# One block for a batch's graph products, and sums of exponentials by accumulating DMAs, in a two-layer graph network on one core

## The chip, the core and the metric

The kernel runs on one core of a Trainium2 chip. A core has TensorE (PE in the profile; its weight loads are PEld), VectorE (DVE), ScalarE (ACT), GpSimd (POOL), SyncE (SP), which here only issues DMAs, and 16 DMA engines that serve the queues of SP, POOL and ACT. The metric is the device time of one launch in microseconds (us), the median of several runs.

## The reference

Inputs are x (16 batches of 1024 nodes with 256 features), an adjacency of 1024 x 1024, and weights, all float32. Layer 0, for each batch, with 4 heads of 64:

```
c_adj = mean over features of x                       # one number per node
A     = | |sigmoid(c_j - c_i) - 0.5| - 0.5 | * 2      # symmetrised
g     = relu(x^T @ (adj * A) * para)                  # 256 x 1024: the queries
k, v  = x @ kv_w
out   = softmax(q k^T * scale) v                      # per head, 1024 x 1024 scores
x     = layernorm(x + out)
```

Layer 1 multiplies by a normalised adjacency, then two linear layers with batch norms and a ReLU, adds x and normalises. Nothing of layer 1 is touched by the change.

## The kernel before, in words

Layer 0 runs over 16 batches. For each batch PE does four kinds of work.

Keys and values. Four steps of values and four of keys, from x transposed.

Graph products. The product of x^T and the weights wg (1024 x 1024, held as eight tiles of 128 rows) is made as a 2 x 2 block product with seven half-size products instead of eight (a Strassen form); batch 0 alone does it plainly. Each of p1 to p7 (line 883) is four matmuls of 128 x 128 by 512, which the profile shows as eight, since each float32 matmul is two instructions. The left factors are sums of quarters of x, kept in two slots of the tile S (`left_first`, `left_third`, `left_last`, lines 849 to 859). The right factors are differences of quarters of wg, made in place by `right(1)` to `right(4)` (line 869), four DVE instructions each, so that a difference must wait until the products that want the old values have read them. Products 1 and 2 accumulate in the PSUM tile pga, 6, 7 and 4 in pgb, 3 in pgd, 5 in pgc; DVE and ACT combine them in qT, weigh them by para and rectify them.

Attention. A batch has 32 units: two pairs of heads, two halves of the queries, eight blocks m of keys. One unit is `scores` (line 1051: matmuls of 64 x 64 into a PSUM tile ps), an exponential on ACT into an SBUF tile p (line 1056, four buffers), and `outputs` (line 1072: matmuls of 64 x 64 that accumulate over the eight m in two PSUM tiles po). `outputs` also adds p to the running sum acc on DVE: line 1080 for the first two, line 1082 for the other six, so seven additions for the eight blocks. After m = 7, ACT copies the first po to oT (line 1089), DVE adds the second (line 1090), DVE transposes oT in blocks of 32 (line 1101), and SP stores it and loads it back in rows (`squares`, `squares_to_rows`).

The end of a batch. For each pair of heads `normalise` sums acc over partitions by matmuls with ones (den, line 1120; shape 128 x 32), ACT copies den (line 1126), and SP stores and reloads it as columns. `residual` takes the reciprocal on DVE (line 1141), multiplies o by it and adds it to x on POOL (lines 1147 and 1148). Then come the statistics of the layernorm on DVE (`statistics_x1`), its application on ACT (`finish_x1`), and a store of x by POOL.

The order is written by hand for PE, ACT, DVE and SP: every instruction of these engines stands in the queue as the program emits it. POOL is ordered by the scheduler. Units go in bursts of two, 16 bursts (u = 0 to 15) to a batch. In each, PE does the scores of this burst, then `back`, the outputs of the burst before; after that comes what is put at that u: at u = 0 seven of the eight key and value steps of the next batch, with the side work for its weights (`weights_abs`, `weights_tanh` on ACT, `weights_adj` on DVE) in between, and den of the batch before's second pair; at u = 4 products 1, 3 and 2 of the next batch, with the last step of its keys; at u = 5 to 7 the differences of the weights (`between`); at u = 8 products 6, 7, 5, 4 with den of the first pair; from u = 9 on, loads and side work for the batch after. `full` holds residuals, `late` the layernorm, `rows_of` the loads of o, `sums` the calls of `normalise`, and `run` emits the next few of a list.

PSUM has three tags with two buffers each: s (ps, two banks a buffer), t (one bank; pga to pgd, keys, values, den) and o (one bank; po). SBUF tiles are in pools; xS is a pool of one buffer for x in squares and, before, for S as well.

Of the kernel before, what the change touches and what calls it, by code (L numbers as in the profile page):

```python
# [515 lines left out]
def fast_path(  # L516
# [216 lines left out]
    with (  # L733
        tc.tile_pool(name="l0c", bufs=1) as l0c,
        tc.tile_pool(name="qkv", bufs=2) as qkv,
        tc.tile_pool(name="pp", bufs=4) as pp,
        tc.tile_pool(name="accp", bufs=2) as accp,
        tc.tile_pool(name="rdp", bufs=1) as rdp,
        tc.tile_pool(name="op", bufs=2) as op,
        tc.tile_pool(name="osp", bufs=1) as osp,  # L740
# [42 lines left out]
        def prologue(b):  # L783
# [65 lines left out]
            def left_first():  # L849
                s2, s4 = s["S"][:, 0], s["S"][:, 1]  # L850
                nc.vector.tensor_tensor(s2, A21, A22, ALU.add)
                nc.vector.tensor_tensor(s2, s2, A11, ALU.subtract)
                nc.vector.tensor_tensor(s4, A12, s2, ALU.subtract)
# [7 lines left out]
            def right(k):  # L861
                for i in KC:
# [38 lines left out]
            def p1():  # L901
                s["qT"] = qkv.tile([P, CC, N], F32, tag="qT", name=f"qT_{b}")
                s["S"] = xsp.tile([P, 2, NCH // 2, P], F32, tag="xS", name=f"S_{b}")
                pg["a"] = tile_t(f"pga_{b}")
                product(1, pg["a"], True)
                nc.scalar.copy(q_at(1, H0), pg["a"])  # L906
                left_first()
                right(1)

            def p3():  # L910
# [3 lines left out]

            def p2():
# [4 lines left out]
            def between(u):  # L920
                right(u - 3)
                if u == 6:
                    nc.vector.tensor_add(q_at(0, H1), q_at(0, H1), q_at(1, H0))
                if u == 7:
                    left_third()

            def p6():
                pg["b"] = tile_t(f"pgb_{b}")
                product(6, pg["b"], True)
                nc.vector.tensor_add(q_at(0, H1), pg["b"], q_at(0, H1))  # L930
                left_last()

            def p7():
                product(7, pg["b"], False)
                nc.vector.tensor_add(q_at(1, H1), pg["b"], q_at(1, H0))

            def p5():
# [6 lines left out]

            def p4():
# [73 lines left out]
            else:  # L1019
                a, t, j = weights_abs, weights_tanh, weights_adj  # L1020
                side += [(f, (n,)) for f, n in (
                    (a, 0), (t, 0), (a, 1), (t, 1), (a, 2), (t, 2), (a, 3),
                    (t, 3), (a, 4), (t, 4), (j, 0), (a, 5), (t, 5), (j, 1),
                    (a, 6), (j, 2), (j, 3), (t, 6), (j, 4), (a, 7), (j, 5),
                    (t, 7), (j, 6), (j, 7),
                )]
            if b:
                s["graph"] = dict(
                    between=between, p=(None, p1, p2, p3, p4, p5, p6, p7),
# [13 lines left out]
        def scores(i):  # L1043
# [11 lines left out]
            p = pp.tile([P, N], F32, tag="p", name=f"p_{i}")  # L1055
# [3 lines left out]
        def outputs(i):  # L1059
# [16 lines left out]
            def sums():  # L1076
                if m == 0:
                    g["p0"] = p
                elif m == 1:
                    nc.vector.tensor_add(g["acc"], g.pop("p0"), p)  # L1080
                else:
                    nc.vector.tensor_add(g["acc"], g["acc"], p)  # L1082

            if i < len(units) - 1:
                sums()
            if m == NCH - 1:
                k = (b * PAIRS + pr) * 2 + qh
                g["oT"] = op.tile([P, HALF], F32, tag="oT", name=f"oT_{k}")
# [49 lines left out]
        def residual(b, pr, qh):  # L1138
# [5 lines left out]
            if (b, pr) != (B - 1, PAIRS - 1):  # L1144
                o = g["o"].rearrange("p n q d -> p n (q d)")
                oh = o.rearrange("p n (h d) -> p n h d", d=D)
                nc.gpsimd.tensor_tensor(oh, oh, r, ALU.mult)  # L1147
                nc.gpsimd.tensor_tensor(xs, xs, o, ALU.add)  # L1148
# [34 lines left out]
        scr = const.tile([P, P], F32, name="scr")  # L1183
# [34 lines left out]
        def adjacency_diagonal():  # L1218
            for n in range(NCH):
# [90 lines left out]
        with tc.manual_schedule(  # L1310
# [70 lines left out]
            for j in range(len(bursts)):  # L1381
# [3 lines left out]
                if u == 0:  # L1385
                    steps, side = next_steps, next_side
                    next_first, next_steps, next_side = [], [], []
                if j:
                    back(j - 1)
                if u in (5, 9, 13):  # L1390
                    run(rows_of, 1)
                if u == 5 and b + 2 < B:
                    load_x(b + 2)
                    next_first, next_steps, next_side = prologue(b + 2)
# [10 lines left out]
                elif u == 0:  # L1405
                    for i in range(7):
                        if b:
                            run(steps, 1)
                            run(side, (2, 3, 2, 3, 2, 2, 99)[i])
# [3 lines left out]
                elif u < 4:  # L1413
                    if u == 1:
                        run(full, 2)
                    else:
                        run(late, 1)
                    run(side, 99)
                elif u == 4:
                    p = st[b + 1]["graph"]["p"]  # L1420
                    keys_last = steps[:1] if b else []
                    del steps[: len(keys_last)]
                    p[1]()
# [625 lines left out]
```

## Time and profile before

| | |
|---|---|
| time, median of 3 runs | 2445.71 us (2445.69 to 2445.86) |
| the profiled execution | 2446.41 us, its span 2444.6 us |
| granted TensorE clock | 0.997 |
| PE busy | 2411.5 us, 99% of the span |
| DVE busy | 1862.8 us, 76% |
| ACT busy | 1238.3 us, 51% |
| POOL busy | 475.7 us, 19% |
| POOL's DMA queue | 50.34 MB, 4.9% of 16 engines |

A line of a group names the line of code, the engine, the operation, what it writes and reads, the shapes and the count; then the busy time and the mean of one in ns; then the idle time of the engine just before, and what ended most of it. A line of the timeline gives the start in us from the span's start, the duration, the engine, line, operation and tiles, how many equal instructions are merged, and in brackets the idle time before with its releaser. The end of a matmul is modelled, so PE's pace is read from one start to the next. Idle time of an engine that is not the bottleneck costs nothing.

### The profile page before, as it was taken

What the parts mean: (1) busy time and instruction counts of PE and PEld (TensorE: products, weight loads), DVE (VectorE), ACT (ScalarE), POOL (GpSimd) and SP (SyncE); (2) the same over time, 40 slices, a digit from 0 to 9 for tenths busy, and PEclk for the clock granted to TensorE, in tenths of its full rate; (3) what the DMA queues carried; (4) which work ended last, traced back from release to release, by engine and by line L of the source; (5) the groups of instructions that cost most, each with busy time, mean ns of one, the idle gap of its engine ahead of it and who ended that gap; (6) DMA issues with size and microseconds to landing.
All of it is one profiled execution on the core that took longest, in us unless ns stands there. A gap on an engine that the chain in (4) does not pass through costs nothing.

```text
span 2444.6 us, 32834 instructions
## 1 busy us (share of the span) xinstructions
PE 2411.5 (99%) x12422; PEld 1029.6 (42%) x12422; DVE 1862.8 (76%) x2570; ACT 1238.3 (51%) x1545; POOL 475.7 (19%) x486
## 2 busy tenths in 40 slices
PE   9999999999999999999999999999999999999997
PEld 5343443443434434434334343344444444444455
DVE  5688878878888888788788888956566566478978
ACT  7376675765765756657647667421110111045568
POOL 0021122111311211122112112422122122010026
PEclk9999999999999999999999999999999999999999
DMA  5124232332232332322322327221222222165559
GB/s 164 40 42 85 57 49 70 70 53 68 38 83 54 48 84 56 53 70 56 63 62 44 83 49 97 82 103 70 96 92 78 94 86 86 69 241 172 172 210 343
DMA packets 423175, 221.99 MB, mean 91 GB/s; under 512 B 361568, under 2 KB 394848, under 8 KB 414560
## 3 DMA queue, kind: packets, MB, share of 16 engines
q1 hardware_dynamic: 417648, 168.94, 28.4%
q0 software_dynamic: 4832, 50.34, 4.9%
q8 instruction: 99, 1.62, 0.3%
q14 instruction: 68, 0.56, 0.1%
q10 hardware_dynamic: 528, 0.52, 0.1%
HBM read 136.06 MB, written 83.69 MB: 90 GB/s over the span
## 4 chain that ended last, share of the span: by engine, by line
PE 86%; DVE 9%; ACT 3%; DMA 1%; issue 1%; POOL 0%; POOLq 0%; DVEq 0%
PE ps L1051 18%; PE po L1072 18%; PE pgb L883 7%; PE b_agg L1556 4%; PE pga L883 4%; PE c_agg L1556 4%; PE pk L980 4%; PE b_o L1763 3%; PE pv L993 3%; PE a_agg L1556 2%; PE b_h L1588 2%; PE pgd L883 2%; PE pgc L883 2%; PE a_o L1763 2%; PE c_o L1763 2%; PE c_h L1588 2%
## 5 line engine op out<-in xcount | busy, mean ns | idle before, releaser
L1056 ACT ACTIVATE p<-ps 128x1024 f32<-128x1024 f32 x512 | 497.6, 1021 | 183.7 <-PE ps L1051 130.1
L1082 DVE TENSOR_TENSOR acc<-acc,p 128x1024 f32<-128x1024 f32 x384 | 500.1, 1302 | 54.2 <-ACT p L1056 29.3
L1051 PE MATMUL ps<-qT,kT 64*64 64x512 f32 x4096 | 488.1, 592 | 0.3 <-ACT p L1056 0.3
L1072 PE MATMUL po<-p,v 64*64 64x512 f32 x4096 | 485.3, 589 | 0.0
L1147 POOL TENSOR_TENSOR o<-o,r_all 128x512 f32<-128x512 f32 x62 | 94.8, 1538 | 1090.8 <-DVE r_all L1141 1052.5
L1072 PEld LDWEIGHTS po<-p,v 64*64 64x64 f32 x4096 | 158.2, 133 | 281.3 <-issue 274.3
L1051 PEld LDWEIGHTS ps<-qT,kT 64*64 64x64 f32 x4096 | 151.4, 133 | 286.8 <-issue 249.2
L834 DVE SCALAR_TENSOR_TENSOR wg<-wg,adj_s 128x1024 f32<-128x1024 f32 x128 | 149.4, 1217 | 16.5 <-ACT wg L830 16.5
L825 ACT ACTIVATE wg<-crow,ccol 128x1024 f32<-128x1024 f32 x128 | 146.8, 1147 | 0.5 <-DMA crow<-c 0.5
L830 ACT ACTIVATE wg<-wg 128x1024 f32<-128x1024 f32 x128 | 136.0, 1062 | 0.9
L980 PE MATMUL pk<-xT,kvw_s 128*128 128x512 f32 x256 | 121.8, 598 | 3.1 <-ACT drow L1126 3.1
L993 PE MATMUL pv<-kvw_s,xT 128*128 128x256 f32 x512 | 124.0, 385 | 0.0
L993 PEld LDWEIGHTS pv<-kvw_s,xT 128*128 128x128 f32 x512 | 94.9, 190 | 50.0 <-issue 13.4
L893 ACT ACTIVATE qT<-qT 128x512 f32<-128x512 f32 x60 | 37.3, 629 | 149.8 <-DVE qT L896 145.2
L883 PE MATMUL pgb<-wg,S 128*128 128x512 f32 x240 | 111.0, 605 | 0.0
L883 PE MATMUL pga<-wg,x 128*128 128x512 f32 x240 | 109.6, 599 | 0.7 <-ACT qT L906 0.7
L1556 PE MATMUL a_agg<-ahT,x1l 128*128 128x512 f32 x240 | 108.1, 593 | 0.7 <-ACT agg L1298 0.7
L1148 POOL TENSOR_TENSOR x<-x,o 128x512 f32<-128x512 f32 x62 | 107.8, 1748 | 2.3
L1556 PE MATMUL b_agg<-aT,x1S 128*128 128x512 f32 x240 | 107.9, 592 | 0.0
L654 ACT COPY p_agg<-a_agg 128x512 f32<-128x512 f32 x15 | 8.8, 586 | 183.3 <-PE a_agg L1556 183.3
L690 POOL TENSOR_TENSOR x1S<-x1l 128x512 f32<-128x512 f32 x15 | 19.0, 1264 | 352.3 <-PE c_agg L1556 349.0
L1080 DVE TENSOR_TENSOR acc<-p,p 128x1024 f32<-128x1024 f32 x64 | 77.4, 1209 | 7.5 <-ACT p L1056 7.5
(230 smaller groups left out, 3511.8 us busy)
## 6 DMA issues: line engine op xcount, KB each, us to landing
h<-hw POOLq DMA_DIRECT2D x16, 2048.0 KB, 6.7
hl<-h SPq DMA_DIRECT2D x32, 1024.0 KB
x<-x POOLq DMA_DIRECT2D x16, 1024.0 KB, 4.2
x1l<-x SPq DMA_DIRECT2D x16, 1024.0 KB
xf<-x SPq DMA_DIRECT2D x16, 1024.0 KB
o<-oS SPq DMA_DIRECT2D x62, 256.0 KB
o<-o SPq DMA_DIRECT2D x248, 64.0 KB
x<-in_x_dram SPq DMA_DIRECT2D x15, 1024.0 KB
```

The source lines that it names most:

```text
L825: nc.scalar.activation(w, s["crow"], AF.Abs, bias=s["ccol"][:, n : n + 1])
L830: nc.scalar.activation(w, w, AF.Tanh, scale=0.5)
L834: nc.vector.scalar_tensor_tensor(w, w, 1.0, adj_s[:, n, :], op0=ALU.subtract, op1=ALU.mult)
L883: nc.tensor.matmul(ps, left, right, start=(start and i == 0), stop=(i == NCH // 2 - 1), skip_group_check=True,)
L980: nc.tensor.matmul(ps, kvw_s[:, c, kc * P : (kc + 1) * P], s["xT"][:, c, hs], start=(c == 0), stop=(c == CC - 1),)
L993: nc.tensor.matmul(pt[:, j * C : (j + 1) * C], s["xT"][:, c, n * P : (n + 1) * P], kvw_s[:, c, C : 2 * C], start=(c == 0), stop=(c == CC - 1),
L1051: nc.tensor.matmul(ps[kh * D : (kh + 1) * D, hd * HALF : (hd + 1) * HALF], kT[r, pr, ks], qT[r, pr, qh * HALF : (qh + 1) * HALF], start=Tr ...
L1056: nc.scalar.activation(p, ps, AF.Exp)
L1072: nc.tensor.matmul(g["po"][kh][hd * D : (hd + 1) * D, :], s["v"][r, m, h * D : (h + 1) * D], p[r, hd * HALF : (hd + 1) * HALF], start=(m = ...
L1082: nc.vector.tensor_add(g["acc"], g["acc"], p)
L1556: nc.tensor.matmul(ps, left, right, start=(start and i == 0), stop=(i == NCH // 2 - 1), skip_group_check=True,)
L1763: nc.tensor.matmul(ps, left, right, start=(start and i == 0), stop=(i == 1), skip_group_check=True,)
```

## The change

It does four things.

- The seven graph products stand in one block at u = 4, in the order 1, 3, 2, 6, 7, 5, 4. The differences that stood at u = 5 to 7 are made in the block, the first sums of x at the end of u = 0, and two of the four differences of `right(1)` at u = 1. pga and pgb take PSUM buffers of the tag o instead of t.
- Of each group's eight tiles p, that of m = 2 lies in a pool of its own (ppb, one buffer) and takes the sums: the tiles of m = 4 and 5 are added to it by DMAs that POOL issues (`accum_op`), and it is added to acc after m = 7. So DVE does five additions in a group instead of seven.
- The residual's multiplication goes from POOL to DVE, and its addition to x is made by an accumulating DMA on POOL's queue.
- Work around these is moved: den of the first pair from u = 8 to u = 9, ahead of that burst's outputs; the load of x for the batch after next and its first step (`begin`, the column sums) from u = 5 and u = 8 to the end of u = 4 and to u = 5; the first pair's residuals from u = 11 to u = 13; the rows of o from u = 13 to u = 15; and the side work for weights is ordered anew. oT gets a pool of one buffer, and a scratch tile shares one with den's row.

```diff
@@ left_first
+                s["S"] = xsp.tile([P, 2, NCH // 2, P], F32, tag="xS", name=f"S_{b}")
                 s2, s4 = s["S"][:, 0], s["S"][:, 1]
@@ right
-            def right(k):
-                for i in KC:
+            def right(k, rows=KC):
+                for i in rows:
@@ the products
-            def p1():
+            def first_three():
                 s["qT"] = qkv.tile([P, CC, N], F32, tag="qT", name=f"qT_{b}")
-                s["S"] = xsp.tile([P, 2, NCH // 2, P], F32, tag="xS", name=f"S_{b}")
-                pg["a"] = tile_t(f"pga_{b}")
+                pg["a"] = tile_o(f"pga_{b}")
                 product(1, pg["a"], True)
                 nc.scalar.copy(q_at(1, H0), pg["a"])
-                left_first()
-                right(1)
-
-            def p3():
+                right(1, KC[2:])
                 pg["d"] = tile_t(f"pgd_{b}")
                 product(3, pg["d"], True)
                 nc.scalar.copy(q_at(0, H1), pg["d"])
-
-            def p2():
+                right(2)
                 product(2, pg["a"], False)
                 nc.vector.tensor_mul(q_at(0, H0), pg["a"], para_s[:, 0, H0])
                 rectify(0, H0)
-            def between(u):
-                right(u - 3)
-                if u == 6:
-                    nc.vector.tensor_add(q_at(0, H1), q_at(0, H1), q_at(1, H0))
-                if u == 7:
-                    left_third()
             def p6():
-                pg["b"] = tile_t(f"pgb_{b}")
+                left_third()
+                right(3)
+                nc.vector.tensor_add(q_at(0, H1), q_at(0, H1), q_at(1, H0))
+                pg["b"] = tile_o(f"pgb_{b}")
                 product(6, pg["b"], True)
                 nc.vector.tensor_add(q_at(0, H1), pg["b"], q_at(0, H1))
                 left_last()
-            def p7():
+                right(4)
+            def last_three():
                 product(7, pg["b"], False)
...
@@ side work of batches from 2 on
-                    (a, 0), (t, 0), (a, 1), (t, 1), (a, 2), (t, 2), (a, 3),
-                    (t, 3), (a, 4), (t, 4), (j, 0), (a, 5), (t, 5), (j, 1),
-                    (a, 6), (j, 2), (j, 3), (t, 6), (j, 4), (a, 7), (j, 5),
-                    (t, 7), (j, 6), (j, 7),
+                    (a, 0), (t, 0), (j, 0), (a, 1), (t, 1), (j, 1), (a, 2), (t, 2),
+                    (a, 3), (t, 3), (j, 2), (a, 4), (t, 4), (a, 5), (j, 3), (t, 5),
+                    (j, 4), (a, 6), (t, 6), (j, 5), (a, 7), (t, 7), (j, 6), (j, 7),
@@ scores
-            p = pp.tile([P, N], F32, tag="p", name=f"p_{i}")
+            pool, tag = (ppb, "pb") if m == 2 else (pp, "p")
+            p = pool.tile([P, N], F32, tag=tag, name=f"p_{i}")
@@ sums, in outputs
+                elif m == 2:
+                    g["pb"] = p
+                elif m in (4, 5):
+                    nc.gpsimd.dma_start(g["pb"], p, accum_op=ALU.add)
                 else:
                     nc.vector.tensor_add(g["acc"], g["acc"], p)
+                if m == NCH - 1:
+                    nc.vector.tensor_add(g["acc"], g["acc"], g.pop("pb"))
@@ residual
-                nc.gpsimd.tensor_tensor(oh, oh, r, ALU.mult)
-                nc.gpsimd.tensor_tensor(xs, xs, o, ALU.add)
+                nc.vector.tensor_tensor(oh, oh, r, ALU.mult)
+                nc.gpsimd.dma_start(xs, o, accum_op=ALU.add)
@@ the bursts
+                if u == 9 and b < B - 1:
+                    run(sums, 1)
                 if j:
                     back(j - 1)
-                if u in (5, 9, 13):
+                if u in ((5, 9, 13) if b == B - 1 else (5, 9, 15)):
                     run(rows_of, 1)
-                if u == 5 and b + 2 < B:
-                    load_x(b + 2)
-                    next_first, next_steps, next_side = prologue(b + 2)
...
-                            run(side, (2, 3, 2, 3, 2, 2, 99)[i])
+                            run(side, (2, 2, 2, 2, 2, 2, 99)[i])
...
+                    st[b + 1]["graph"]["left"]()
                 elif u == 4:
                     p = st[b + 1]["graph"]["p"]
...
+                    p[0]()
                     run(late, 2)
...
+                    p[1]()
+                    if b:
+                        run(steps, 1)
+                    p[2]()
+                    if b + 2 < B:
+                        load_x(b + 2)
+                        next_first, next_steps, next_side = prologue(b + 2)
+                elif u < 4:
+                    if u == 1:
+                        run(full, 2)
+                        st[b + 1]["graph"]["right"](1, range(2))
+                    else:
+                        run(late, 1)
+                elif u == 5:
+                    run(next_first, 1)
+                elif u > 8:
...
-                    if u == 11:
-                        run(full, 2)
...
+                    if u == 13:
+                        run(full, 2)
...
-                    run(next_side, 1)
+                    run(next_side, 2 if u in (11, 13) else 1)
```

More of the change, by code (lines that the diff above doesn't have):

```diff
@@ L736, in fast_path @@
         tc.tile_pool(name="pp", bufs=4) as pp,
+        tc.tile_pool(name="ppb", bufs=1) as ppb,
         tc.tile_pool(name="accp", bufs=2) as accp,
@@ L739, in fast_path @@
         tc.tile_pool(name="op", bufs=2) as op,
+        tc.tile_pool(name="otp", bufs=1) as otp,
         tc.tile_pool(name="osp", bufs=1) as osp,
@@ L931, in p6 @@
                 left_last()
-            def p7():
+                right(4)
+            def last_three():
                 product(7, pg["b"], False)
                 nc.vector.tensor_add(q_at(1, H1), pg["b"], q_at(1, H0))
-            def p5():
                 pg["c"] = tile_t(f"pgc_{b}")
@@ L943, in p5 @@
                     weigh(c, H1)
-            def p4():
                 product(4, pg["b"], False)
@@ L1028, in prologue @@
                 s["graph"] = dict(
-                    between=between, p=(None, p1, p2, p3, p4, p5, p6, p7),
+                    left=left_first, right=right, p=(first_three, p6, last_three),
                 )
@@ L1087, in outputs @@
                 k = (b * PAIRS + pr) * 2 + qh
-                g["oT"] = op.tile([P, HALF], F32, tag="oT", name=f"oT_{k}")
+                very_last = k == 4 * B - 1
+                pool, tag = (op, "o") if very_last else (otp, "oT")
+                g["oT"] = pool.tile([P, HALF], F32, tag=tag, name=f"oT_{k}")
                 nc.scalar.copy(g["oT"], g["po"][0])
@@ L1182, in fast_path @@
         rows, diag, colsum, deg, dinv = dg[:, 0], dg[:, 1], dg[:, 2], dg[:, 4], ncol[:, 0, :NCH]
-        scr = const.tile([P, P], F32, name="scr")
         def load_weights():
@@ L1218, in adjacency_diagonal @@
         def adjacency_diagonal():
+            scr = rdp.tile([P, P], F32, tag="drow", name="scr")
             for n in range(NCH):
@@ L1412, in fast_path @@
                             run(rows_of, 1)
-                elif u < 4:
-                    if u == 1:
-                        run(full, 2)
-                    else:
-                        run(late, 1)
-                    run(side, 99)
+                    st[b + 1]["graph"]["left"]()
                 elif u == 4:
                     p = st[b + 1]["graph"]["p"]
-                    keys_last = steps[:1] if b else []
-                    del steps[: len(keys_last)]
-                    p[1]()
-                    run(keys_last, 1)
+                    p[0]()
                     run(late, 2)
-                    p[2]()
-                    p[3]()
-                elif u == 8:
-                    p = st[b + 1]["graph"]["p"]
-                    p[6]()
-                    run(next_first, 1)
-                    run(sums, 1)
                     if b == B - 2:
@@ L1436, in fast_path @@
                             adjacency_rows(n)
-                    p[7]()
-                    p[5]()
-                    p[4]()
-                elif u < 8:
-                    st[b + 1]["graph"]["between"](u)
-                else:
+                    p[1]()
[14 more added lines that the diff above has]
+                elif u > 8:
                     if u == 9 and b + 2 < B:
                         load_squares(b + 2, 0)
-                    if u == 11:
-                        run(full, 2)
                     if u == 12:
```

## The prediction

> **What bounds the kernel now.** I read the page first, then the timelines of PE and ACT around one graph block, then the releases behind PE's few gaps. The page: busy time by engine, and two groups.
>
> ```profile
> PE 2411.5 (99%) x12422; PEld 1029.6 (42%) x12422; DVE 1862.8 (76%) x2570; ACT 1238.3 (51%) x1545; POOL 475.7 (19%) x486
> ...
> L1082 DVE TENSOR_TENSOR acc<-acc,p 128x1024 f32<-128x1024 f32 x384 | 500.1, 1302 | 54.2 <-ACT p L1056 29.3
> L1147 POOL TENSOR_TENSOR o<-o,r_all 128x512 f32<-128x512 f32 x62 | 94.8, 1538 | 1090.8 <-DVE r_all L1141 1052.5
> L1148 POOL TENSOR_TENSOR x<-x,o 128x512 f32<-128x512 f32 x62 | 107.8, 1748 | 2.3
> ```
>
> PE is busy for 2411.5 of 2444.6 us. DVE has 582 us spare, so work taken off it pays only where PE now waits for it. Next, PE's timeline in the seventh batch, then ACT's over the same microseconds.
>
> ```profile
> 656.75 1.90 PE L1051 MATMUL ps<-qT,kT 64*64 64x512 f32 x16
> 658.47 1.90 PE L1072 MATMUL po<-p,v 64*64 64x512 f32 x16
> 660.30 3.70 PE L883 MATMUL pga<-wg,x 128*128 128x512 f32 x8
> 663.83 1.88 PE L980 MATMUL pk<-xT,kvw_s 128*128 128x512 f32 x4
> ...
> 684.58 1.90 PE L1072 MATMUL po<-p,v 64*64 64x512 f32 x16
> 686.40 3.70 PE L883 MATMUL pgb<-wg,S 128*128 128x512 f32 x8
> 690.04 1.06 PE L1120 MATMUL den<-acc,ones 128*32 128x512 f32 x8
> 691.03 3.70 PE L883 MATMUL pgb<-wg,S 128*128 128x512 f32 x8
> ```
>
> ```profile
> 658.41 1.03 ACT L1056 ACTIVATE p<-ps 128x1024 f32<-128x1024 f32 x1 [2.05 <-DVE acc L1082]
> 659.74 1.02 ACT L1056 ACTIVATE p<-ps 128x1024 f32<-128x1024 f32 x1 [0.30 <-DVE acc L1082]
> 660.66 0.58 ACT L1089 COPY oT<-po 128x512 f32<-128x512 f32 x1
> ...
> 686.53 0.59 ACT L1089 COPY oT<-po 128x512 f32<-128x512 f32 x1 [0.62 <-PE po L1072]
> ```
>
> A product of the graph (8 matmuls) lasts 3.43 us, a start each 0.429; a unit's scores or outputs 0.86. PE runs through without a gap; it loses time only where the tile shape changes. By the starts, the step from po (64x64) to pga (128x128) is 0.519 where 0.429 is usual, and the second matmul after it comes 0.533 after the first: 0.194 for entering. Leaving (pgd to ps) shows 0.522 and a second start 0.03 late: 0.124. A batch takes 96.69 us, and about 1.5 of it is of this kind. The other fact is in ACT's lines: the copy that empties the first po bank ends at 661.24, when pga has been running for 0.94 us. Today nobody waits for it, because pga lies in a bank of its own. One more gap recurs in 14 batches: PE at pk, for the copy of den.
>
> ```profile
> 637.65 1.14 ACT L825 ACTIVATE wg<-crow,ccol 128x1024 f32<-128x1024 f32 x1
> 638.69 0.57 ACT L1126 COPY drow<-den 128x512 f32<-128x512 f32 x1
> ```
> ```profile
> 639.32 1.12 PE L980 MATMUL pk<-xT,kvw_s 128*128 128x512 f32 x2 [0.23 <-ACT drow L1126]
> ```
>
> **What the Trainium skill says.** TensorEngine Tiling (Array Packing), Key Properties: changing the tiling mode drains TensorE. The trace agrees: 0.09 at the step, 0.03 to 0.10 at the next. DMA: Bandwidth & Descriptors, Anatomy of one DMA: a transfer issued from GpSimd costs about 2.0 us plus bytes over 436 GB/s. The trace's 1 MB store of x (POOL) lands after 4.24 us (formula 4.4), the 2 MB store of h after 6.6. The same page, Two DMAs through the same engine are not ordered: a second DMA on the same bytes must wait for the first one's semaphore. So the two accumulations into pb run one after the other. Collectives: The Full Stack, The bandwidth ceiling: a reducing transfer reads two sources and got half the rate of a copy (32 against 62 GB/s). No run here shows an accumulating DMA.
>
> **The change, part by part** (batches 0 to 14 have a graph block).
>
> 1. One block instead of two. One entry and one exit go: 0.194 + 0.124 = 0.318, times 15: **-4.8**.
>
> 2. den of the first pair leaves the block (0.093 in, 0.093 + 0.104 out = 0.29) and goes between scores and outputs of the tenth burst. The last batch has it there already: 0.09 in, 0.093 + 0.03 out = 0.21. Times 15: **-1.2**.
>
> 3. pga and pgb go to the tag of po, whose two banks hold the group just finished. The first product cannot start before ACT has copied po's first bank. In the seventh batch that copy ends 0.94 us after pga starts now, 0.71 where ACT is not behind (686.53 + 0.59 against 686.40), and PE starts 0.05 after a release (drow 639.26, pk 639.32). So PE stands 0.76 to 1.0 us at each block. What would hide it, the next burst's scores, comes after the block. pgb needs the second bank, freed by DVE (L1090) some 4 us later, but is first written three products in, at 10.3: hidden. I take 0.85, since DVE has two sums fewer to be behind with: 15 x 0.85 = **+12.8**.
>
> 4. The differences of weights and rows (L869, 0.61 us each when chained) move from bursts 6 to 8 into the block. DVE enters at most 5.2 us after its start (oS ends at 665.57); right(1)'s rest and right(2), 6 x 0.61, end near 9.5, and the fourth product wants them at 10.3. Then DVE waits for the third product's end (10.4), multiplies, and runs left_third, right(3), two additions: 8 operations, 5.0 us, to 15.5. The fifth product (P7) overwrites pgb and may start then; PE gets there after P6 and the keys at 13.7 + 1.7 = 15.4. So 0.1 x 14, and 1.8 in batch 0, which has no keys left: **+3.3**. left_last and right(4) end by 19, ahead of 18.9 + 0.43 and 22.3: hidden. left_first, now ahead of the second burst, lies beside the key and value products.
>
> 5. The weights' order at the batch's start: ahead of drow's copy ACT has three activations (t3, a4, t4) where it had four (t3, a4, t4, a5), one of 1.14 us less. The 0.23 gap (0.174 of pitch and a 0.104 hitch) goes: 14 x 0.28 = **-3.9**.
>
> 6. Sums: DVE loses m = 2, 4, 5 and gains one addition of pb, so 2 x 1.30 x 64 = 167 us less, off the path. POOL gets two DMAs of 512 KB per group. Take t = 0 at the scores of m = 4. Its exponential ends at 2.17; the first DMA lands at 2.2 + L, the second at 2.3 + 2L. Wanted: p's buffer for the next group's second exponential (four in rotation; natural start 8.9), and pb added before L1090, so that the next group's outputs find both banks at 12.0: 2.3 + 2L + 1.25 + 0.65 + 0.05 under 12.0, L under 3.8. A plain copy by the trace's line through 1 and 2 MB is 1.9 + 1.17 = 3.1: no wait. At half the rate 1.9 + 2.34 = 4.2 (estimate from that line and the skill's half): 12.65 against 12.0 at the bank, 0.65 at two groups of a batch (the other two have a block behind them), and up to 1.1 with the buffer. Below nothing it cannot be: PE gains nothing from DVE's slack here. I take **0** in the forecast, and up to +50 for the range.
>
> 7. Residual: POOL's 1.54 and 1.75 us go, DVE gets 0.69 (x62, as L1090) ahead of which it waits for o and the reciprocals; xs grows by a DMA in 512-byte runs. The statistics a burst (3.43 us) later wait for it; DVE already waits 1.16 us there for POOL. If it lands after 5 us, DVE is 1.5 us later, and the buffers of p catch that while it has two sums less: **0**.
>
> 8. SP: the load of x moves behind the block's last product in program order. The x it overwrites is stored after eight activations (4.7 us), which now follow the third product: 12 + 4.7 + 4.3, then 5.6 for the load (675.75 to 681.3 now) ends 27 us into the block; csum (2.28, DVE) asks at about 28.7. Hidden with under 2 us to spare; late, it holds all sums queued on DVE. At the tenth burst SP has den and dcol (about 5 us), then o, then the squares, which so come one to two bursts later; their 128-byte packets run beside the third group's accumulations: a risk for item 6.
>
> Sum: -4.8 - 1.2 + 12.8 + 3.3 - 3.9 = **+6.2** on a span of 2444.6 (the profiled run took 2446.41, 0.7 above the median shown). On the median 2445.71: **2452**, 0.25% slower; own range 2449 to 2458.
>
> **The rivals.** Accumulations land late (0.32): L near 4.2. For it, the two source reads; against it, that SBUF is both source and target. 31 groups at 0.65 give +20; with the buffer's wait, which also delays the copy of item 3 by 1.2, about +50: 2464 to 2505, 2478 in the middle. Late and crowded (0.08): the third and fourth groups share the engines with the squares and o, L over 5: 2520.
>
> Not slower (0.13): the wait of item 3 is at its floor. Place: the copy at the block's head. If the exponentials ahead of it no longer wait for DVE (2.05 and 0.30 above) it costs 0.76, 11.4 in all, and if DVE also reaches P7 in time, 1.4 more goes: +3.4, 2449. It decides at 0.77 us per block, where the sum crosses 4.9 us. Faster (0.05): the same, with entries that lose their 0.104 hitch, (1.6) comes to +1.8; it takes something that I do not see.
>
> **How the numbers follow.** 0.2% is 4.9 us, about what a measurement of this kernel can tell from no change. Forecast 0.42, of which 0.12 lies under 2450.6. Same: 0.13 + 0.12 = 0.25. Slower: 0.30 + 0.32 + 0.08 = 0.70. Faster 0.05. The range 2444 to 2500 leaves out the 0.05 below and the crowded case with the end of the late one, about 0.15.
>
> **What the profile after would show.** One graph block of 28 products' matmul pairs per batch, its first matmul released by ACT's copy of po after 0.8 to 1.0 us (item 3); PE at pk without drow (5); P7 released by DVE within 0.2 (4); p's DMAs landing in 3.1 us and no PE wait behind L1090 or an exponential (6). I am wrong if these land near or over 4 us, if DVE waits for x at csum, or if the copy is no wait at all.

## The result, and the profile after

The changed kernel takes 3022.94 us (median of 4 runs, 3020.63 to 3023.78) against 2445.72 for the kernel before: 1.2358 times as long, with a 95% interval of 1.2337 to 1.2380. Slower was right. The size, 577 us where 6 were forecast and 54 was the end of the range, was not.

The page of the kernel after: busy time by engine, three of the groups, and the two accumulating DMAs (KB of one, then the median us from issue to landing).

```profile
PE 2557.5 (85%) x12422; PEld 1062.3 (35%) x12422; DVE 1735.8 (57%) x2504; ACT 1241.7 (41%) x1545; POOL 453.5 (15%) x552
...
L1047 ACT ACTIVATE p<-ps 128x1024 f32<-128x1024 f32 x512 | 507.8, 1023 | 710.2 <-DMA p<-p 528.0
L1079 DVE TENSOR_TENSOR acc<-acc,p 128x1024 f32<-128x1024 f32 x64 | 78.4, 1225 | 432.1 <-DMA p<-p 432.0
...
L886 PE MATMUL pga<-wg,x 128*128 128x512 f32 x240 | 144.2, 756 | 187.3 <-ACT oT L1088 187.3
...
p<-p POOLq DMA_DIRECT2D x128, 512.0 KB, 5.4
...
x<-o POOLq DMA_DIRECT2D x62, 256.0 KB, 5.5
```

DVE is less busy, as the change wants (1735.8 us, 1862.8 before). But PE has fallen from 99% of the span to 85%, and the two engines behind it wait for the new DMAs: ACT 528.0 us ahead of its exponentials, DVE 432.0 us ahead of the addition of pb. The same DMAs take 5.4 us from issue to landing, where the forecast had 3.1.

How a wait of ACT comes to PE is seen at the block of the seventh batch. PE's timeline, with its idle time in brackets, then ACT's.

```profile
873.29 1.90 PE L1063 MATMUL po<-p,v 64*64 64x512 f32 x16
888.17 5.31 PE L886 MATMUL pga<-wg,x 128*128 128x512 f32 x8 [12.98 <-ACT oT L1088]
```
```profile
877.37 1.02 ACT L1047 ACTIVATE p<-ps 128x1024 f32<-128x1024 f32 x1 [5.03 <-DMA p<-p]
886.62 1.02 ACT L1047 ACTIVATE p<-ps 128x1024 f32<-128x1024 f32 x1 [8.23 <-DMA p<-p]
887.54 0.58 ACT L1088 COPY oT<-po 128x512 f32<-128x512 f32 x1
```

ACT's queue is in order. The second exponential of the next group wants the buffer of p that the second DMA is still reading, so it stands for 8.23 us; the copy that empties po is queued behind it, and the block is queued on PE behind that copy. PE stands 12.98 us. The row of pga above shows the sum of this over 15 blocks, 187.3 us. Two more of PE's waits (total, times, longest) make up nearly all the rest of its idle time:

```profile
PE ps L1041 <- ACT p L1047: 149.7, 36, 5.9
PE den L1119 <- DVE v L989: 72.6, 14, 7.2
```

The first are scores behind exponentials that wait for a DMA. The second come from the wait of DVE: the addition of pb stands in its queue, ahead of the copy of v that den's place in PSUM waits for (at the start of the seventh batch DVE waits 7.01 us for the DMA, and PE then 4.67 at den). Two more waits at den, for pb's addition itself, add 14.3 us.

POOL's timeline over the same microseconds, and at the next group of that batch, shows why the second DMA is so late.

```profile
868.33 2.60 POOL L1147 DMA_DIRECT2D x<-o  x2 [26.81 <-DVE r_all L1140]
869.93 1.92 POOL L1075 DMA_DIRECT2D p<-p  x1
877.21 1.11 POOL L591 TENSOR_SCALAR rs_l<-mv_l 128x8 f32<-128x8 f32 x1 [5.37 <-DVE mv_l L619]
878.41 2.69 POOL L593 TENSOR_TENSOR rs_l<-rs_l,mhalf 128x8 f32<-128x8 f32 x1
...
881.94 0.92 POOL L1075 DMA_DIRECT2D p<-p  x1 [0.22 <-issue]
```
```profile
922.84 0.87 POOL L1075 DMA_DIRECT2D p<-p  x1 [16.28 <-ACT p L1047]
929.71 0.87 POOL L1075 DMA_DIRECT2D p<-p  x1 [6.00 <-DMA p<-p]
```

In the first group the first DMA is issued right behind two residual DMAs and lands at 877.26, after 7.33 us. The second is then held by four small operations of the layernorm on POOL, which wait for DVE's statistics: issued at 881.94, landed at 886.51, after 4.57. In the second group nothing stands in POOL's queue, and it is late all the same: the scores of m = 4 start at 919.52, the first DMA goes out 3.3 us later and lands at 928.82, the second goes out 0.9 after that and lands at 935.73, 16.2 us after the scores.

Last, the same block in stretches: us, busy time by engine (with counts), granted TensorE clock, DMA share, GB/s.

```profile
862.80:875.50 12.70, 12.39 (x116) 4.03 (x108) 10.82 (x23) 5.87 (x6) 3.51 (x3) 1.00 0.50 66
875.50:888.30 12.80, 0.13 (x1) 0.13 (x1) 5.23 (x11) 2.52 (x3) 5.17 (x5) 0.59 0.31 58
888.30:900.00 11.70, 11.70 (x24) 5.19 (x25) 5.19 (x8) 1.17 (x2) 0.00 (x0) 0.87 0.06 22
```

The clock falls to 0.59 while PE stands and is still below 1 after it (0.87 on average in the third stretch): the first four steps between matmuls are 1.015, 0.854, 0.853 and 0.710 us where 0.429 is usual. The Trainium skill describes this (TensorE: Matmul & The Clock Gate, What's actually happening): after an idle window of about 3.4 us the array gets half its clock pulses, until it has been busy for as long again. The trace agrees, with half pace for about 3 us after this long stand. Outside such stretches the DMAs do not slow the matmuls: 710 of the steps within graph products in this kernel are 0.42 to 0.44 us as before, and 56 about 0.85.

Over layer 0's attention as a whole (first scores to the first product of layer 1), PE's idle time ahead of matmuls, in gaps over 0.05 us, is added up from the trace; the rest is work, at the clock granted. Each kernel's span is within 10 us of what these differences say, so they are where the time is.

| | stage, us | idle, us | gaps over 2 us | rest, us | clock |
|---|---|---|---|---|---|
| before | 1496.8 | 4.1 | 0 | 1492.7 | 1.00 |
| after | 2066.9 | 429.4 | 64 | 1637.5 | 0.887 |
| after without the DMAs of p (next section) | 1523.8 | 25.9 | 2 | 1497.9 | 0.998 |

### The profile page after: what moved, and what is told of

It is laid out like the page before. It is cut to its first block, busy times and chain, and to the rows that moved or that the text cites. A ratio compares the mean times of both kernels' runs of the same rounds, so it can differ in the third digit from the quotient of the medians.

```text
span 3021.4 us, 32826 instructions
## 1 busy us (share of the span) xinstructions
PE 2557.5 (85%) x12422; PEld 1062.3 (35%) x12422; DVE 1735.8 (57%) x2504; ACT 1241.7 (41%) x1545; POOL 453.5 (15%) x552
## 4 chain that ended last, share of the span: by engine, by line
PE 42%; DMA 19%; issue 16%; DVE 10%; ACT 4%; POOL 2%; SPq 2%; POOLq 0%; ACTq 0%; DVEq 0%
DMA p<-p 13%; PE pgb L886 5%; PE pga L886 4%; PE b_agg L1549 4%; PE c_agg L1549 3%; PE ps L1041 3%; ACT p L1047 3%; DMA x<-o 3%; PE po L1063 3%; PE b_o L1756 2%; PE a_agg L1549 2%; PE b_h L1581 2%; DMA o<-o 2%; PE pgc L886 2%; PE c_o L1756 2%
## 5 line engine op out<-in xcount | busy, mean ns | idle before, releaser
L1047 ACT ACTIVATE p<-ps 128x1024 f32<-128x1024 f32 x512 | 507.8, 1023 | 710.2 <-DMA p<-p 528.0
L1041 PE MATMUL ps<-qT,kT 64*64 64x512 f32 x4096 | 528.3, 623 | 149.8 <-ACT p L1047 149.7
L1063 PE MATMUL po<-p,v 64*64 64x512 f32 x4096 | 518.5, 620 | 1.1 <-DVE oT L1089 1.1
L1079 DVE TENSOR_TENSOR acc<-acc,p 128x1024 f32<-128x1024 f32 x64 | 78.4, 1225 | 432.1 <-DMA p<-p 432.0
L886 PE MATMUL pga<-wg,x 128*128 128x512 f32 x240 | 144.2, 756 | 187.3 <-ACT oT L1088 187.3
L1077 DVE TENSOR_TENSOR acc<-acc,p 128x1024 f32<-128x1024 f32 x192 | 233.4, 1216 | 80.6 <-ACT p L1047 72.6
L1075 POOL DMA_DIRECT2D p<-p x128 | 131.0, 1023 | 862.5 <-ACT p L1047 575.2
L1147 POOL DMA_DIRECT2D x<-o x62 | 81.4, 1552 | 542.6 <-DVE r_all L1140 470.1
L886 PEld LDWEIGHTS pga<-wg,x 128*128 128x128 f32 x240 | 57.5, 247 | 271.3 <-ACT oT L1088 200.6
L984 PE MATMUL pv<-kvw_s,xT 128*128 128x256 f32 x512 | 142.0, 426 | 0.0
L1119 PE MATMUL den<-acc,ones 128*32 128x512 f32 x248 | 61.0, 1030 | 86.8 <-DVE v L989 72.6
L872 DVE TENSOR_TENSOR wg<-wg,wg 128x512 f32<-128x512 f32 x120 | 78.9, 688 | 72.3 <-PE pgd L886 72.3
```

The lines of the kernel that those rows point to most:

```text
L886: nc.tensor.matmul(ps, left, right, start=(start and i == 0), stop=(i == NCH // 2 - 1), skip_group_check=True,)
L984: nc.tensor.matmul(pt[:, j * C : (j + 1) * C], s["xT"][:, c, n * P : (n + 1) * P], kvw_s[:, c, C : 2 * C], start=(c == 0), stop=(c == CC - 1),
L1041: nc.tensor.matmul(ps[kh * D : (kh + 1) * D, hd * HALF : (hd + 1) * HALF], kT[r, pr, ks], qT[r, pr, qh * HALF : (qh + 1) * HALF], start=Tr ...
L1047: nc.scalar.activation(p, ps, AF.Exp)
L1063: nc.tensor.matmul(g["po"][kh][hd * D : (hd + 1) * D, :], s["v"][r, m, h * D : (h + 1) * D], p[r, hd * HALF : (hd + 1) * HALF], start=(m = ...
L1075: nc.gpsimd.dma_start(g["pb"], p, accum_op=ALU.add)
```

## The experiments

My theory after the result: nearly all of it is the accumulations of p, through landings that come later than wanted, and half-pace matmuls after each stand. The rivals: the block itself costs far more than was summed (items 3 and 4); the residual's DMA does it (item 7), by crowding POOL's queue; or each DMA costs PE time whatever its deadline.

| kernel | median, us | ratio to before, 95% interval |
|---|---|---|
| block alone | 2559.58 | 1.0463 (1.0449 to 1.0478) |
| block, DMA of the residual | 2547.26 | 1.0414 (1.0398 to 1.0430) |
| block, DMAs of p | 3050.15 | 1.2467 (1.2448 to 1.2486) |
| before, DMAs of p | 2881.11 | 1.1778 (1.1760 to 1.1796) |
| before, DMA of the residual | 2455.32 | 1.0033 (1.0021 to 1.0046) |
| after, no sums of m = 4 and 5 | 2476.26 | 1.0122 (1.0106 to 1.0137) |
| the same, pga in the tag t | 2466.49 | 1.0079 (1.0063 to 1.0094) |
| after, plain copies for accumulations | 2616.30 | 1.0693 (1.0673 to 1.0712) |
| after, one DMA a group | 2653.19 | 1.0841 (1.0825 to 1.0858) |
| after, POOL in program order | 2967.09 | 1.2126 (1.2107 to 1.2145) |
| after, DMAs of m = 1 and 3 | 2943.71 | 1.2007 (1.1971 to 1.2043) |
| before, one early DMA a group | 2563.69 | 1.0468 (1.0450 to 1.0486) |
| after, one early DMA a group | 2718.30 | 1.1095 (1.1076 to 1.1115) |
| before, new order of the weights' work | 2441.90 | 0.9981 (0.9973 to 0.9988) |
| the same, den at the tenth burst | 2463.08 | 1.0067 (1.0054 to 1.0081) |

### The DMAs apart from the block

The block alone puts seven additions back on DVE and the residual's addition on POOL:

```diff
-                elif m == 2:
-                    g["pb"] = p
-                elif m in (4, 5):
-                    nc.gpsimd.dma_start(g["pb"], p, accum_op=ALU.add)
                 else:
                     nc.vector.tensor_add(g["acc"], g["acc"], p)
-                if m == NCH - 1:
-                    nc.vector.tensor_add(g["acc"], g["acc"], g.pop("pb"))
...
-                nc.vector.tensor_tensor(oh, oh, r, ALU.mult)
-                nc.gpsimd.dma_start(xs, o, accum_op=ALU.add)
+                nc.gpsimd.tensor_tensor(oh, oh, r, ALU.mult)
+                nc.gpsimd.tensor_tensor(xs, xs, o, ALU.add)
```

> The changed kernel with both kinds of accumulating DMA undone (all seven sums on DVE, the residual on POOL): the one block and the moved work alone. Theory DMA (the loss comes from the accumulations of p, each over 4.5 us, two in series, which hold p's buffers and the sum pb): 2440 to 2458, my steps 1 to 5 give 2452. Theory block (PE's wait for po's bank at the block's head, and DVE's work crowded into the block, is the loss by itself): over 2600, with the 12 us wait before pga still there.

It takes 114 us more than before, a miss. The block is not nearly free when DVE keeps its sums. The seventh batch's first group, DVE, then ACT, then POOL:

```profile
692.50 2.09 DVE L871 TENSOR_TENSOR wg<-wg 128x512 f32<-128x512 f32 x2
694.51 4.27 DVE L1071 TENSOR_TENSOR acc<-acc,p 128x1024 f32<-128x1024 f32 x2
```
```profile
692.49 1.94 ACT L1045 ACTIVATE p<-ps 128x1024 f32<-128x1024 f32 x2 [2.71 <-DVE acc L1069]
696.66 1.02 ACT L1045 ACTIVATE p<-ps 128x1024 f32<-128x1024 f32 x1 [2.23 <-DVE acc L1071]
```
```profile
692.64 2.84 POOL L1138 TENSOR_TENSOR o<-o,r_all 128x512 f32<-128x512 f32 x2 [22.80 <-DVE r_all L1132]
695.45 4.45 POOL L1139 TENSOR_TENSOR x<-x,o 128x512 f32<-128x512 f32 x2
```

The change put the first sums of x and two differences of right(1) into the first bursts, ahead of the group's sums. While POOL runs its two-input operations, two differences take 2.09 us (1.25 elsewhere) and two sums 4.27 (2.52). The exponentials wait for the sums to free buffers of p, the copy of po is late by the same queue as above, and PE waits 2.24 us at this block. The other three mixes undo one of the two:

> The changed kernel with the sums of p back on DVE, the residual's accumulating DMA kept. Theory DMA: within 20 us of the run with the block alone, since 5.5 us per residual ends about when the statistics want it. Theory residual (its 512-byte runs crowd POOL's queue and make the statistics, then everything on DVE, late): at least 100 us above it.

> The changed kernel with the residual back on POOL, the accumulations of p kept. Theory DMA: 2850 to 2980, most of the loss stays; the part that goes is the first group's, whose first DMA no longer stands behind two residuals on POOL. Theory residual: below 2600.

> The kernel before with the accumulations of p alone (two blocks, residual on POOL as before). Theory DMA: 2750 to 2950, as the pairs are late in all four groups of a batch; somewhat under the changed kernel since pga does not wait for po's bank here. Theory block, or a loss that needs both: below 2520.

The residual's DMA on the block saves 12 us, although POOL then runs no two-input operation beside these sums: the slow additions are the smaller part, and the miss of the block stays. (With two additions fewer on DVE it is 71 us less: 2476 in the next section.) With p's DMAs the block takes 3050, so the DMA of the residual is not the culprit; putting its work back on POOL cost 27 more. The DMAs of p alone, on the old order, take 435 us: the expected size, and on the block 476 (2547 to 3023). So the accumulations of p account for most of the result wherever they stand, and the rival of item 7 falls. The residual's DMA alone, on the old order:

> The kernel before with the residual's multiplication on DVE and its addition by an accumulating DMA, nothing else. DVE's additions beside POOL's two-input operations take up to 2.1 us where 1.2 is usual, and POOL has none left: DVE is less behind, but PE does not wait for DVE here: 2443 to 2452. If the statistics' wait for a 5.5 us DMA reaches PE: over 2460.

It costs 8 us, between the two values expected: small, with a sign that depends on what else DVE and POOL hold at that place.

The kernel before with p's DMAs alone gives the cleanest view of a late pair, since its DMAs land after 4.5 us (median of 128; the least is 4.48). PE, POOL, then ACT, in the second group of the seventh batch, whose scores of m = 4 start at 838.66:

```profile
838.66 1.90 PE L1053 MATMUL ps<-qT,kT 64*64 64x512 f32 x16
840.38 1.90 PE L1075 MATMUL po<-p,v 64*64 64x512 f32 x16
...
855.20 3.70 PE L885 MATMUL pgb<-wg,S 128*128 128x512 f32 x8 [1.28 <-DVE qT L932]
```
```profile
841.98 0.86 POOL L1087 DMA_DIRECT2D p<-p  x1 [10.35 <-ACT p L1059]
847.00 0.87 POOL L1087 DMA_DIRECT2D p<-p  x1 [4.16 <-DMA p<-p]
```
```profile
851.60 1.02 ACT L1059 ACTIVATE p<-ps 128x1024 f32<-128x1024 f32 x1 [3.88 <-DMA p<-p]
```

The first goes out at 3.3: the outputs of m = 2, which read the tile it writes, are the first half of the second line of PE and are done at 841.42. The profile names the last exponential, that of m = 5, but this DMA does not read its tile, and that of m = 4 was done at 840.85. The kernel with plain copies (below) decides it: its first copy writes no tile that PE reads, and in 32 of 64 groups it goes out less than 3 us after the scores, at the earliest after 2.4; here none goes out before 3.3. The DMA lands at 846.47, the second goes out 0.5 later and lands at 851.50, 12.8 after the scores; the exponential that was to start at 8.9 starts at 12.9. That is 4.0 us late with nothing else in POOL's queue. Sixty-four such delays would make 259 us, but not each reaches PE in full: here half a graph block follows on PE, which waits only 1.28 us in it. This kernel's stage has 314 us of idle time and 119 at reduced pace, with POOL's residual and layernorm ahead of other pairs.

### The block without the DMAs of p

```diff
                 elif m in (4, 5):
-                    nc.gpsimd.dma_start(g["pb"], p, accum_op=ALU.add)
+                    pass
```

> The changed kernel with the sums of m = 4 and 5 left out altogether (two of the eight blocks are missing from the denominators): DVE has its relief, and no DMA of p is late. Theory DMA: all that p's accumulations cost goes, 2445 to 2475 (my steps 1 to 5 said 2452). Theory crowded DVE: over 2500, since the block alone with all sums on DVE took 2560.

2476.26, just past the upper end of what was expected: the change without p's DMAs costs 30 us, with them 577. This is the other measure of their part, 547 us: by the table of the stage 403 of idle time and 140 at reduced pace. It also shows items 1 to 5 of the forecast without these DMAs. PE's timeline at the start of the seventh batch, at its block, and at the last block:

```profile
645.76 1.99 PE L971 MATMUL pk<-xT,kvw_s 128*128 128x512 f32 x4 [0.36 <-ACT drow L1125]
...
667.62 3.70 PE L886 MATMUL pga<-wg,x 128*128 128x512 f32 x8 [0.69 <-ACT oT L1088]
...
1466.93 5.12 PE L886 MATMUL pgb<-wg,S 128*128 128x512 f32 x8 [2.58 <-DVE qT L924]
```

The first product waits 0.69 us for ACT's copy (0.76 by the start). To price that wait by itself, pga went back to the tag t:

```diff
-                pg["a"] = tile_o(f"pga_{b}")
+                pg["a"] = tile_t(f"pga_{b}")
```

> The changed kernel without the sums of m = 4 and 5 (missing from the denominators), and pga back in a PSUM buffer of the tag t. My step 3 alone: the wait for po's bank goes, 0.76 at each of 15 blocks, 2463 to 2466. If the tag t makes another wait (keys or pgc for pga's buffer): 2470 or more.

2466.49, just past the upper end of what was expected: about 10 us less, 0.65 a block. The wait at the block's head is real, and of the size of item 3.

### What a DMA costs, and what makes it late

> The changed kernel with the two accumulations replaced by plain copies of p to two scratch arrays in HBM (their sums are missing from the denominators): the same bytes of p read on the same queue, no second source, and neither waits for the other nor the sum for them. Theory half rate: a copy lands in 3.0 to 3.5 us alone where the accumulation took 4.5, and the time is within 60 us of the kernel without these sums. Theory queue (POOL's issue and the crowd on the engines make it late, whatever the operation): it lands in over 4.3 us and the time stays above 2650.

The edit lets the two DMAs write a scratch in HBM instead of adding to pb:

```diff
-                    nc.gpsimd.dma_start(g["pb"], p, accum_op=ALU.add)
+                    nc.gpsimd.dma_start(sink[m - 4], p)
```

2616.30 is neither of the two values expected. Of 512 KB, a plain copy to HBM lands after 2.92 us at best, where an accumulation within SBUF needs 4.48: the forecast's two estimates, 3.1 and 4.2, were near both. How much of the difference is the addition, and how much the other destination, is not shown; no run has a plain copy within SBUF. Beside other traffic, each other's included, the copies took up to 9.2 (median 5.3), and the kernel is 140 us slower than without them, although no copy waits for the other. So lateness is not of accumulation alone; crowded transfers hold the buffers of p as well.

```diff
-                elif m in (4, 5):
+                elif m == 4:
                     nc.gpsimd.dma_start(g["pb"], p, accum_op=ALU.add)
```

> The changed kernel with the sum of m = 5 back on DVE, the accumulation of m = 4 kept. Theory series (a single DMA of 5.4 us fits ahead of p's reuse 5.7 us after its exponential, the second one behind it does not): 2480 to 2620. Theory per DMA (each costs its share): about 2785, half of what the pair costs over the run without them.

2653.19 is between the two theories' values. One DMA a group, with no chain behind it, still costs 177 us over none. Not all of that is the DMA's, since DVE also has one addition more here, and two more cost 71 us (2547 against 2476). Its landings had a median of 6.4 us, close to the 6.2 of the first DMA of a pair in the kernel after. A second DMA in place of DVE's addition makes the other 370.

> The changed kernel with POOL's queue in program order too: nothing else differs than that the first group's second accumulation stands ahead of the layernorm's four small POOL operations and not behind them. Theory queue: that DMA is issued some 4.7 us earlier in each of 15 batches and PE's wait at the block's head shrinks by as much, 2940 to 2965. Theory landing time alone: the queue's order costs nothing, 3010 to 3025.

The edit adds POOL to the engines whose order is written by hand. In each batch's first group the second DMA then stands ahead of the four layernorm operations. Waits of PE for ACT's copy in this kernel (total, times, longest), which were 187.3 us in the kernel after:

```profile
PE pga L886 <- ACT oT L1088: 134.8, 15, 11.0
```

The time falls by 56 us, to just past the upper end of what was expected, and this wait by 52.5: 3.5 a block. This place in POOL's queue is a part of the lateness, a tenth of the whole.

> The changed kernel with the accumulations moved ahead in the group: the tile of m = 0 takes the sums, those of m = 1 and 3 are added to it by DMAs, and it is added to acc ahead of m = 6; as many DMAs, and as many additions on DVE. Theory deadline (a DMA costs what it is late by, and each has now 5.8 us from its exponential to its tile's next use, and the pair 9.3 to the sum): most of the loss goes, 2480 to 2650. Theory per DMA (traffic, ports and queue cost PE whatever the place): above 2900.

Here the tile of m = 0 takes the sums, and m = 1 and 3 are added to it by DMA. 2943.71 is the value expected of a cost per DMA, but it does not decide between the two, since the DMAs did not come early: a DMA may only write that tile once the outputs of m = 0 have read it, so POOL waited 752 us in all for outputs. In the seventh batch the first DMA goes out only with the scores of m = 4 and the second lands 11.6 us after them; and the buffers that they hold are wanted earlier than in the change, by the exponentials of m = 5 and 7 of the same group. A single early DMA (m = 3 onto the tile of m = 0, added to acc after m = 6) was to have the deadline met:

> The kernel before with one accumulation per group, of m = 3 into the tile of m = 0, added to acc after m = 6. It is issued when the outputs of m = 0 have read their tile, lands about 4.6 us later, and m = 7 wants m = 3's buffer about then or later. Theory deadline: 2444 to 2462. Theory per DMA: the pairs cost this kernel 435 us, 3.4 each, so 64 of them about 2660.

> The changed kernel with the same single accumulation per group (one more addition on DVE than in the run without these sums). Theory deadline: only the groups with residual DMAs ahead on POOL are late, by some 2 us: 2490 to 2560. Theory per DMA: as the single accumulation of m = 4, about 2650.

On the old order it costs 117 us, between the deadline's value and the one for a cost per DMA; on the block it is worse than either (242 over none, with one addition more on DVE). The landings were not the 4.6 us I had assumed but 5.65 in the median and up to 9.4. In the trace of the first of the two, the stage is 115 us longer than before: 78 of it is idle time of PE and 37 reduced pace. Nearly all of the idle time has two places; the third line is a wait of DVE (total, times, longest):

```profile
PE ps L1053 <- ACT p L1059: 43.6, 33, 4.7
PE den L1131 <- DVE v L1000: 35.3, 14, 3.4
DVE xT L821 <- DMA xS<-in_x_dram: 54.4, 16, 4.5
```

At the scores PE stands behind exponentials, most of which wait for a DMA of p. At den it stands behind DVE, and DVE waits for something else: a load of x by SP's queue. Just ahead of the seventh batch this load and an accumulation are issued within half a microsecond (659.41 and 659.87), and from 662 to 664 SP's queue moves 0.01 MB, POOL's 0.39. DVE waits 3.49 us for the load, with sums, the addition of pb among them, queued behind it. In the kernel before this wait is 4.3 us in all, at the kernel's start. So another transfer is late here beside an accumulation; in the kernel before with pairs of DMAs DVE waits 49.8 us for the same load. That is a price that the accumulation's own deadline does not show, though no run changes it alone; and since no run had all landings early enough, it stays open whether an accumulation with room would be free. More buffers of p would have been the direct trial; it was not made.

### The order of the weights' work, and den

Item 5 by itself, on the kernel before:

```diff
-                            run(side, (2, 3, 2, 3, 2, 2, 99)[i])
+                            run(side, (2, 2, 3, 3, 2, 2, 99)[i])
```

> The kernel before with one activation of the side work moved behind den's copy at the start of a batch (two, two, three, three side steps instead of two, three, two, three). My step 5: the wait of keys for den's bank goes, 14 x 0.28, 2441.8. If the wait only moves to another copy on ACT: 2445.7 or a little more.

2441.90, as expected: the wait for den's copy is gone and the stage is 5.3 us shorter, its idle time 1.0 instead of 4.1. It is the one version that beats both kernels, by 4.3 us or 0.19% (0.12 to 0.27).

> The kernel before with the side work reordered as in the run of that alone, and den of the first pair at the tenth burst ahead of its outputs. My step 2: 1.2 less than with the side work alone, 2440.7. If den then waits for acc, or its bank for another: 2442 or more.

Moving den to the tenth burst on top of that loses 21 us, where 1.2 were to be gained. At u = 8 den stands between products 6 and 7 and covers DVE's addition to pgb's result (L930), so that product 7 may overwrite pgb. Without it PE waits there, up to 0.8 us in each of 15 blocks (total, times, longest); one wait of 4.1 us of the outputs for DVE in the last batch comes on top, and the rest of the stage is 7 us longer:

```profile
PE pgb L883 <- DVE qT L930: 11.8, 15, 0.8
```

The change itself has a step of the keys at that place, and doesn't lose this cover.

## Why the prediction was right or wrong

**Item 6, the sums by DMA: this is the step that failed.** It took 0, with up to +50 for the range; it is +547 over the same kernel without those DMAs. Four of its terms were short. The time of a DMA: 3.1 was chosen, 4.48 is the least and 5.4 the median; the half-rate estimate of 4.2, which I had and gave to a rival, was the nearer one. The first start: 2.2 left out that the DMA writes a tile which PE's outputs of m = 2 read; it is 3.3. The second start: 2.3 + 2L left 0.1 us from the first landing to the next issue; it is mostly 0.5, and up to 0.9 where POOL holds nothing else. And POOL's queue: I summed the DMAs as if POOL were free, while the residual's DMAs, or four operations waiting for DVE, stand ahead of a pair. With the first three and L = 4.5 the second landing is 3.3 + 4.5 + 0.5 + 4.5 = 12.8, against 8.9 for the exponential: 4 us late even where POOL is free and nothing is crowded. Even with L = 3.1 it would have been 10.0. I had written the exponential's bound down and then priced the range by the bank's, which came later, at "up to 1.1 with the buffer". By my own 2.3 + 2L the exponential's bound is passed at L = 3.3, not 3.8, and at 4.2 it is late by 1.8.

The step also had no term for what a stand does. It passes through ACT's queue, from the exponential to the copy behind it, and through DVE's, from the addition of pb to what den waits for, to PE (187, 150 and 87 us at the block, the scores and den); and after a long stand matmuls run at half pace for some microseconds. Reduced pace is 140 of the 547 us. The rival "late and crowded" had this mechanism's beginning, at 2520; its price was too small by the same terms.

**Item 3, the banks: right.** 0.76 us a block by the trace, the floor that I gave, and about 10 us for 15 blocks by the run with the other tag; 12.8 was forecast. In the kernel after itself the same wait is 187.3 us, since the copy is late there.

**Item 4, differences in the block: right in kind.** (0.1 x 14 and 1.8 are 3.2, not 3.3.) Product 7 starts 0.20 late in a usual batch (0.1 forecast) with a second step 0.1 late, and 1.92 in batch 0 (1.8). Missed: in the last block sixteen small operations of the adjacency's diagonal stand ahead on DVE, and product 7 waits 2.58 us and then runs at half pace, 4.3 in all. That left_first is hidden holds only while DVE has sums less to do: with seven sums the block costs 114 us.

**Item 5, the wait at pk: wrong.** It was to go; it is 0.36 in the kernel without p's DMAs, where 0.23 was before. I counted ACT's activations ahead of den's copy. Those ahead of the copy of kT don't count, because ACT waits there for PE anyway; after it two activations, 1.15 and 1.06 us, still stand ahead of den's copy, and that copy ends as PE starts. On the old kernel, another order of this work won the 4 us.

**Items 1 and 2, fewer switches of the tile shape.** The trace of the kernel without p's DMAs has one entry and one exit per block (second start 0.533 and first 0.522 in place of 0.429) and den between scores and outputs, as forecast; their 6 us were not measured by a run of their own. Together with items 3 to 5 a batch takes 97.6 us there, 0.9 more than before, about 14 in 15 batches. Most of the rest of that kernel's 30 us lies in single places: batch 0, the last block, and a wait of 4.5 us in the last batch (with half pace after it 6.0), where DVE's transposes wait for a load of the adjacency ahead of the oT that PE wants.

**Item 7, the residual: 0 was forecast**; 8 us on the old order, a gain of 12 on the block with the sums on DVE. **Item 8, SP's queue:** no wait for x at csum shows beyond the 6.5 us at the kernel's start, which is also there before.

## What to carry to other kernels

A sum that moves from an engine to a DMA moves into a chain: write down the latest start (who still reads the target), the issue, the transfer as accumulation, the issue behind it, the landing, and hold it against the earliest buffer that is wanted back, not the last. What is late by its own chain is late in every turn of the loop, and what stands in order behind the waiting instruction can carry it to the critical engine, with some microseconds of half pace on top. Look also at which loads of other queues it will run beside. And before a small piece of work is moved because it only costs a switch, look at what it covers where it is.

## What was not expected of the hardware

- In the kernel after, an accumulating DMA of 512 KB within SBUF takes 4.48 us at least and 10.4 at most; in the kernel with plain copies, one of that size to HBM takes 2.92 at least. The residual's of 256 KB in 512-byte runs, issued two at a time, takes 4.3 to 8.3, so little less for half the bytes.
- A DMA that waits for another's landing is mostly issued 0.53 us after it (0.3 to 0.9 where POOL holds nothing else), and its issue occupies POOL for 0.87 us (0.57 for a plain copy; medians).
- In the one stretch looked at (kernel before with one early DMA, 662 to 664 us), POOL's queue with an accumulation moved 0.39 MB, and SP's, with loads under way, 0.01 MB.
- With the block alone, DVE's additions of 128x1024 take 2.1 us each instead of 1.26 while POOL runs an operation with two inputs; the Trainium skill names the contention (GPSIMD Engine Reference, Specifications), without a figure.
- The length of a gap alone does not tell whether half pace follows. Ahead of product 7 of the last block PE stands 2.58 us in the kernel without p's DMAs, and steps of 1.015, 0.854, 0.853 and 0.517 us follow; in the kernel after it stands 2.59 us at the same place, and the steps from the second on are 0.43. With the block alone, gaps of 2.24 us at the block's head were followed by half pace in 6 of 13 batches; gaps of 0.7 never were.
